# Queueing transposes ahead at the ends of the layers of a four-layer graph network, and halving its last output

## The chip, the cores and the metric

The kernel runs on one core of one Trainium2 chip. The metric is the device time of one launch, in microseconds (us). Three runs of the kernel before took 530.57, 530.88 and 531.29 us. A core has engines that run side by side, each through a queue of instructions of its own in a fixed order, and wait for one another on semaphores: TensorE (PE in the profile) multiplies matrices into PSUM, DVE (VectorE) and ACT (ScalarE) do elementwise work, GpSimd (POOL) also, and SyncE (SP) issues most DMAs.

## The reference

A graph of 512 nodes with 512 features each and 16384 edges goes through four layers, each of the form x = x + layer(relu(layernorm(x))). In short:

```python
h = relu(layernorm(x));  x = x + transformer(h, edges)        # layer 0
h = relu(layernorm(x))
x = x + h @ wc + mean_over_edges(h @ wn) + bias               # layer 1
h = relu(layernorm(x))
for e in range(4):                                            # layer 2, experts; top 2 of 4 are kept
    t = relu(A @ h @ Wl[e, 0] + bl[e, 0] + h @ Wr[e, 0])      # A: mean over incoming edges
    t = relu(A @ t @ Wl[e, 1] + bl[e, 1] + t @ Wr[e, 1])
    x = x + gate[e] * t
h = relu(layernorm(x))
x = x + relu(S @ (h @ W + b))                                 # layer 3, S: normalized adjacency with loops
```

All of it is float32. The edge sums are done as products with a dense 512 x 512 matrix of edge counts.

## The kernel before

The nodes lie in four blocks of 128 rows, one row to a partition: `xs` holds x, `h` the normalized rows. A product of `h` with a weight needs `h` transposed, so `turn` (L189) transposes a block on TensorE, four pieces of 128 x 128 into one PSUM bank (L193), and ACT copies the bank into `hT` (L194). All four layers use the one `hT`.

In layer 0 the order of TensorE, DVE and ACT is written out by hand (`manual_schedule`, L480 to L695). Its end is `ff_up(1, 6)`, then the down projections `ff_down` of blocks 2 and 3 (banks `pf22`, `pf23`, L690 to L695), the residual sums on DVE (L381) and the normalizations `norm2_a`, `norm2_b`, `norm2_c` (L433 to L445). The PSUM pools are `ps_mm` and `ps_x`; `banks` says from which the next bank is taken. From L702 on there is one pool of eight banks.

In layers 1 and 3 a scheduler orders the instructions of each engine from the order in the program and the dependences. In layer 2, from L956 on, only TensorE's order is by hand.

Layer 1 (L736 to L754): for blocks 0 and 1, then for 2 and 3, two turns, then `pbe` = h @ wn for both (its high part is cast by ACT, L709, its low part is left by DVE, L710), then `pal` = h @ wc for both (added to `xs` on DVE, L747). GpSimd adds the bias to `xs` (L739). Then four edge sums `psu` (L751), each followed by an add on DVE (L752), a normalization `norm_relu` (DVE and ACT, L158 to L184), and a low part `hs` (L754).

Layer 2 begins with, for each block, a turn, the gate product `pg` (L764) and eight products `pag` for the edge sums of `h` (L767). Sums of quarters of `hT`, of the edge sums and of the weights follow on DVE (`right_sums`, `left_sums`), for a scheme that makes a 2 x 2 block product from seven multiplications (`seven`). Weights are loaded by SP into five buffers, each as soon as its last reader is done. The last expert ends, for each block, with `po` (L950), `close` (an edge sum `pq` on TensorE, an add on DVE L907, a relu on ACT L909, an add into `xs` on DVE L910) and `norm_relu`.

Layer 3 (L978 to L1004): for each block a turn, `ph` = h @ W (L985), bias on DVE (L987), a scaled high part and a scaled whole on ACT (L989, L990), the low part on DVE (L991). Then the edge sums `pm` of all four blocks over source blocks 0 to 2 and then over 3 (L997), and for each block a relu on ACT (L1001), an add on DVE (L1003) and the output DMA on SP (L1004). `rm` and `o` are in pools of two buffers each.

Of the kernel before, what the change touches and what calls it, by code (L numbers as in the profile page):

```python
# [8 lines left out]
F32 = mybir.dt.float32  # L9
F16 = mybir.dt.float16  # L10
BF16 = mybir.dt.bfloat16
R = mybir.dt.float32r
I32 = mybir.dt.int32
AF = mybir.ActivationFunctionType
ALU = mybir.AluOpType
# [3 lines left out]
P = 128  # L19
N = 512  # L20
D = 512
E = 16384
NB = N // P
KB = D // P
# [4 lines left out]
NX = 4  # L29
# [7 lines left out]
def fast(  # L37
# [4 lines left out]
    nc = tc.nc  # L42
# [4 lines left out]
    rows = ctx.enter_context(tc.tile_pool(name="rows", bufs=2))  # L47
    ps_mm = tc.alloc_tile_pool(name="ps_mm", bufs=2, space=PSUM)
    ps_lo = tc.alloc_tile_pool(name="ps_lo", bufs=2, space=PSUM)
    ps_sc = tc.alloc_tile_pool(name="ps_sc", bufs=1, space=PSUM)  # L50
    banks = [(ps_mm, "mm"), (ps_mm, "mm"), (ps_lo, "lo")]
    taken = [0]

    def bank(name):
        pool, tag = banks[taken[0] % len(banks)]
        taken[0] += 1
        return pool.tile([P, 512], F32, tag=tag, name=name)
# [5 lines left out]
    xs = const.tile([P, NB, D], F32, name="xs")  # L63
# [34 lines left out]
    gw = const.tile([P, KB, NX], F32, name="gw")  # L98
# [22 lines left out]
    ident = const.tile([P, P], F32, name="ident")  # L121
# [9 lines left out]
    h = const.tile([P, NB, D], F32, name="h")  # L131
    hT = const.tile([P, KB, N], F32, name="hT")
# [53 lines left out]
    def norm_relu(blocks, name, first=None):  # L186
        norm_relu_end(blocks, name, norm_relu_begin(blocks, name), first)

    def turn(dst_t, src_t, b, name):  # L189

        p = bank(f"tp_{name}{b}")
        for k in range(KB):
            nc.tensor.transpose(p[:, k * P:(k + 1) * P], src_t[:, b, k * P:(k + 1) * P], ident)  # L193
        nc.scalar.copy(dst_t[:, :, b * P:(b + 1) * P], p.rearrange("p (k n) -> p k n", k=KB))  # L194

    def mm(p, pairs):
        for i, (a, c) in enumerate(pairs):
            nc.tensor.matmul(p, a, c, start=(i == 0), stop=(i == len(pairs) - 1))  # L198

    def blk(t, k, j):  # L200
        return t[:, k, j * P:(j + 1) * P]
# [16 lines left out]
    C = deg_p.tile([P, NB, N], R, name="C")  # L218
# [5 lines left out]
    W = N // 2  # L224
# [199 lines left out]
    def ff_up(hf, f):  # L424
        ff_up_out(hf, f, ff_up_mm(hf, f))
# [53 lines left out]
    ET = mybir.EngineType  # L479
    with tc.manual_schedule(engines={ET.PE, ET.DVE, ET.Activation}):  # L480
# [25 lines left out]
        for c in range(NCH):  # L506
# [16 lines left out]
            i, at = divmod(c - 17, 9)  # L523
            if 0 <= i < len(first):
                w, t, off, j, cols = first[i]
# [98 lines left out]
        p = ff_up_mm(0, 2)  # L624
# [8 lines left out]
        ps_x = tc.alloc_tile_pool(name="ps_x", bufs=4, space=PSUM, reuse_waits="tile")  # L633
# [4 lines left out]
        p = ff_up_mm(0, 6)  # L638
# [39 lines left out]
        p = ff_up_mm(1, 0)  # L678
# [8 lines left out]
        nc.vector.reciprocal(ideg_b, ideg_b)  # L687
        ff_up(1, 4)
        ff_up(1, 6)
        p2, p3 = bank("pf22"), bank("pf23")  # L690
        ff_down(2, p2, range(FB))
        y = residual(p2, 2, "y2")
# [14 lines left out]
    def split(hi, lo, full, copy):  # L707

        copy(hi, full)  # L709
        nc.vector.tensor_sub(lo, full, hi.bitcast(F32))  # L710
# [22 lines left out]

    pair = main.tile([P, 2, NB, D], F32, tag="pair", name="pair")
    beta = pair.bitcast(R)
    for blocks in ((0, 1), (2, 3)):  # L736
        for b in blocks:
            turn(hT, h, b, "h2_")
            nc.gpsimd.tensor_add(xs[:, b, :], xs[:, b, :], bias1_b)  # L739
        for b in blocks:  # L740
            p = bank(f"pbe{b}")
            mm(p, [(blk(hT, k, b), wns[:, k, :]) for k in range(KB)])
            split(beta[:, 0, b, :], beta[:, 1, b, :], p, nc.scalar.copy)
        for b in blocks:
            p = bank(f"pal{b}")
            mm(p, [(blk(hT, k, b), wcs[:, k, :]) for k in range(KB)])
            nc.vector.tensor_add(xs[:, b, :], p, xs[:, b, :])  # L747
    hs = main.tile([P, 2, NB, D], R, tag="hs", name="hs")
    for b in range(NB):
        p = bank(f"psu{b}")  # L750
        mm(p, [(blk(CT, j, b), beta[:, i, j, :]) for j in range(NB) for i in range(2)])  # L751
        nc.vector.scalar_tensor_tensor(xs[:, b, :], p, icnt[:, b:b + 1], xs[:, b, :], op0=ALU.mult, op1=ALU.add)  # L752
        norm_relu((b,), "n2_", hs[:, 0, b, :])
        nc.vector.tensor_sub(hs[:, 1, b, :], h[:, b, :], hs[:, 0, b, :].bitcast(F32))  # L754

    ct_p.release()
    te_p = ctx.enter_context(tc.tile_pool(name="te_p", bufs=1, side="right", reuse_waits="tile"))
# [1 line left out]

    pg = bank("pg")  # L760
    pag = [bank(f"pag{k}") for k in range(KB)]
    for b in range(NB):
        turn(hT, h, b, "h3_")
        mm(pg[:, b * NX:(b + 1) * NX], [(blk(hT, k, b), gw[:, k, :]) for k in range(KB)])  # L764
        for k in range(KB):
            for i in range(2):
                nc.tensor.matmul(pag[k], blk(hs[:, i, :, :], b, k), C[:, b, :], start=(b == 0 and i == 0),  # L767
                                 stop=(b == NB - 1 and i == 1))

# [132 lines left out]
    def close(e, b, t, zz, gt):  # L904
        q = bank(f"pq{e}_{b}")
        mm(q, [(blk(C, a, b), zz[:, i, a, :]) for a in range(NB) for i in range(2)])
        nc.vector.scalar_tensor_tensor(t, q, ideg[:, b:b + 1], t, op0=ALU.mult, op1=ALU.add)  # L907
        r = rows.tile([P, D], F32, tag="r1", name=f"re{e}_{b}")
        nc.scalar.activation(r, t, AF.Relu, scale=gt[:, b, e:e + 1])  # L909
        nc.vector.tensor_add(xs[:, b, :], xs[:, b, :], r)  # L910
# [3 lines left out]
    def outer(e, w, gt):  # L914
        wl, wr, bl_b = w
        eT = eTs[e]
        L = left_sums(eT, scratch[:, 0:3], scratch[:, 3])

        zz = main.tile([P, 2, NB, D], R, tag="hs", name=f"zz{e}")

        def result_z(i, j, value):
            v = value(None)
            hi, lo = (zz[:, g, 2 * i:2 * i + 2, j * W:(j + 1) * W] for g in range(2))
            split(hi, lo, v, nc.scalar.copy)

        seven(f"pz{e}", [(L, wl)], copied, result_z)
        te = te_p.tile([P, NB, D], F32, tag="te", name=f"te{e}")
        if e < NX - 1:
            bias = [bl_b[:, None, j * W:(j + 1) * W].to_broadcast([P, 2, W]) for j in range(2)]

            def first_o(p):
                ts = []
                for j in range(2):
                    t = uu.tile([P, 2, W], F32, tag="u", name=f"u_b{e}_{j}")
                    nc.vector.tensor_add(t, p, bias[j])
                    ts.append(t)
                return ts

            def result_o(i, j, value):
                t = te[:, 2 * i:2 * i + 2, j * W:(j + 1) * W]  # L940
                if (i, j) == (0, 0):
                    nc.vector.tensor_add(t, value(None), bias[0])
                else:
                    value(t)

            seven(f"po{e}", [(L, wr)], first_o, result_o)
        for b in range(NB):
            if e == NX - 1:
                p = bank(f"po{e}_{b}")
                mm(p, [(blk(eT, k, b), wr[:, k, :]) for k in range(KB)])  # L950
                nc.vector.tensor_add(te[:, b, :], p, bl_b)
            close(e, b, te[:, b, :], zz, gt)
            if e == NX - 1:
                norm_relu((b,), "n3_")

    with tc.manual_schedule(engines={ET.PE}):  # L956
        a0, a1 = weights0(0), weights0(1)
# [14 lines left out]
        w3 = load_w(W3, "w3")  # L972
        b3_b = load_bc(b3, "b3_b")
        outer(3, o3, gt)

    for b in range(NB):  # L978
        nc.vector.tensor_add(blk(C, b, b), blk(C, b, b).bitcast(F32), ident)
        nc.vector.tensor_scalar(xs[:, b, :], xs[:, b, :], nanf[:, b:b + 1], None, op0=ALU.add)  # L980
    gs = main.tile([P, 2, NB, D], R, tag="hs", name="gs")
    for b in range(NB):
        turn(hT, h, b, "h4_")
        p = bank(f"ph{b}")
        mm(p, [(blk(hT, k, b), w3[:, k, :]) for k in range(KB)])  # L985
        t = rows.tile([P, D], F32, tag="r0", name=f"th{b}")
        nc.vector.tensor_add(t, p, b3_b)  # L987
        gg = rows.tile([P, D], F32, tag="r1", name=f"gg{b}")
        nc.scalar.activation(gs[:, 0, b, :], t, AF.Copy, scale=isd[:, b:b + 1])  # L989
        nc.scalar.activation(gg, t, AF.Copy, scale=isd[:, b:b + 1])  # L990
        nc.vector.tensor_sub(gs[:, 1, b, :], gg, gs[:, 0, b, :].bitcast(F32))  # L991
    pm = [bank(f"pm{b}") for b in range(NB)]
    for a in ((0, 1, 2), (3,)):
        for b in range(NB):
            for c in a:
                for i in range(2):
                    nc.tensor.matmul(pm[b], blk(C, c, b), gs[:, i, c, :], start=(c == 0 and i == 0),  # L997
                                     stop=(c == NB - 1 and i == 1))
    for b in range(NB):
        r = rows.tile([P, D], F32, tag="r1", name=f"rm{b}")  # L1000
        nc.scalar.activation(r, pm[b], AF.Relu, scale=isd[:, b:b + 1])  # L1001
        o = rows.tile([P, D], F32, tag="r0", name=f"o{b}")
        nc.vector.tensor_add(o, r, xs[:, b, :])  # L1003
        nc.sync.dma_start(out[b * P:(b + 1) * P, :], o)  # L1004


    ps.release()

# [429 lines left out]
```

## Time and profile before

| what | value |
|---|---|
| runs, median | 530.88 us |
| the profiled execution's own time | 528.97 us |
| its span in the profile | 527.2 us |
| TensorE busy | 482.4 us, 92% |
| DVE busy | 358.2 us, 68% |
| ACT busy | 154.9 us, 29% |
| GpSimd busy | 8.3 us, 2% |
| chain that ended last, by engine | PE 70%, DVE 20%, ACT 5%, DMA 2%, issue 2% |

The span runs from the first to the last instruction in the profile; the run's own time has a little more around it. The profile cuts the span into 40 slices and gives the busy tenths of each engine in each (9 is 90% or more), and the clock that TensorE was granted. A timeline lists the instructions of an engine in order: start, duration, engine, line, operation, output and input, shapes, and in brackets how long the engine had been idle before and which instruction ended that. The ends of matmuls are modelled, and pipelined groups overlap a little, so steps are best measured from start to start. Layer 1 begins at 207.66 us, layer 2 at about 248, its experts' products at 262.04, layer 3 at 488.76.

### The profile page before, as it was taken

What the parts mean: (1) busy time and instruction counts of PE and PEld (TensorE: products, weight loads), DVE (VectorE), ACT (ScalarE), POOL (GpSimd) and SP (SyncE); (2) the same over time, 40 slices, a digit from 0 to 9 for tenths busy, and PEclk for the clock granted to TensorE, in tenths of its full rate; (3) what the DMA queues carried; (4) which work ended last, traced back from release to release, by engine and by line L of the source; (5) the groups of instructions that cost most, each with busy time, mean ns of one, the idle gap of its engine ahead of it and who ended that gap; (6) DMA issues with size and microseconds to landing.
All of it is one profiled execution on the core that took longest, in us unless ns stands there. A gap on an engine that the chain in (4) does not pass through costs nothing.

```text
span 527.2 us, 5637 instructions
## 1 busy us (share of the span) xinstructions
PE 482.4 (92%) x2159; PEld 358.0 (68%) x2159; DVE 358.2 (68%) x726; ACT 154.9 (29%) x315; POOL 8.3 (2%) x14
## 2 busy tenths in 40 slices
PE   2999889696999998999999999999999999999791
PEld 1798556354774673446888888888888888875451
DVE  8898999998987868818564457823783256558521
ACT  3886443332521321212402121112202120223421
POOL 2000000000000000100000000000000000000000
PEclk9999999989999999999999999999999999999997
DMA  7820202200003054112004042203131040000002
GB/s 250 287 75 1 80 2 79 80 21 0 1 22 119 0 171 149 60 63 98 0 1 159 1 159 81 80 1 129 43 104 45 6 154 0 1 1 0 1 2 83
DMA packets 18354, 34.42 MB, mean 65 GB/s; under 512 B 1512, under 2 KB 1808, under 8 KB 18320
## 3 DMA queue, kind: packets, MB, share of 16 engines
q1 hardware_dynamic: 17504, 32.61, 18.4%
q10 hardware_dynamic: 816, 1.38, 0.7%
q8 instruction: 19, 0.31, 0.2%
q14 instruction: 15, 0.12, 0.1%
HBM read 32.93 MB, written 1.05 MB: 64 GB/s over the span
## 4 chain that ended last, share of the span: by engine, by line
PE 70%; DVE 20%; ACT 5%; DMA 2%; issue 2%; ACTq 0%; DVEq 0%
PE pe_b L805 8%; PE pff L198 5%; PE pe_a L805 5%; PE pe_c L805 5%; PE pq L198 5%; PE pz_b L805 3%; PE po_b L805 3%; PE pbe L198 3%; PE pqk L198 3%; PE pwo L377 3%; PE pf L430 3%; PE pal L198 3%; DVE m L304 2%; PE ph L198 2%; PE pz_a L805 2%; PE po_a L805 2%
## 5 line engine op out<-in xcount | busy, mean ns | idle before, releaser
L811 DVE TENSOR_TENSOR u_pe<-pe_b,u_first 128x512 f32<-128x512 f32 x12 | 8.3, 692 | 53.6 <-PE pe_b L805 53.6
L198 PE MATMUL pq<-zz,C 128*128 128x512 f32 x128 | 33.1, 412 | 0.0
L271 DVE TENSOR_SCALAR ohs<-iota_h,src_f,dw_i 128x256 bf16<-128x256 f16 x104 | 28.9, 340 | 1.7 <-PE cps L273 1.6
L198 PE MATMUL pff<-hT,w 128*128 128x256 f32 x128 | 28.6, 381 | 0.7 <-issue 0.7
L198 PEld LDWEIGHTS pq<-zz,C 128*128 128x128 f32 x128 | 24.1, 188 | 7.2 <-issue 1.9
L273 PE MATMUL cps<-ohs,ohd 128*128 128x256 bf16 x104 | 19.5, 289 | 9.7 <-DVE ohs L271 9.7
L430 PE MATMUL pf<-w,ffT 128*128 128x512 f32 x64 | 28.1, 592 | 0.0
L909 ACT ACTIVATE re<-te,gt 128x512 f32<-128x512 f32 x16 | 11.6, 723 | 54.9 <-DVE te L907 54.9
L871 ACT ACTIVATE eT<-u_pe,vecs 128x256 f32<-128x256 f32 x24 | 10.9, 500 | 56.4 <-DVE u_pe L811 56.4
L198 PEld LDWEIGHTS pff<-hT,w 128*128 128x128 f32 x128 | 24.1, 190 | 5.0 <-issue 1.7
L273 PEld LDWEIGHTS <-ohd 128*128 128x128 f16 x128 | 15.7, 145 | 13.6 <-DVE ohd L266 7.9
L299 PE MATMUL psc<-qT,kT 64*128 64x256 f32 x128 | 17.8, 421 | 4.2 <-DVE s L310 4.2
L430 PEld LDWEIGHTS pf<-w,ffT 128*128 128x128 f32 x64 | 12.0, 190 | 13.9 <-issue 13.6
L304 DVE TENSOR_REDUCE m<-psc 128x256 f32<-128x2048 f32 x8 | 18.3, 2286 | 1.7 <-PE cps L273 1.2
L310 DVE TENSOR_TENSOR s<-psc,m 128x1024 f32<-128x1024 f32 x16 | 18.8, 1216 | 0.1
L348 PE MATMUL aps<-s,v 128*64 128x256 f32 x128 | 15.8, 390 | 3.0 <-DVE nt_l L145 3.0
L299 PEld LDWEIGHTS psc<-qT,kT 64*128 64x128 f32 x128 | 13.2, 204 | 7.8 <-issue 6.5
L709 ACT CAST zz<-u_pz 128x512 fp32r<-128x512 f32 x12 | 7.4, 618 | 37.7 <-DVE u_pz L811 37.7
L338 DVE TENSOR_TENSOR s<-s,r 128x2048 f32<-128x2048 f32 x8 | 18.3, 2286 | 0.1
L198 PE MATMUL ph<-w,hT 128*128 128x512 f32 x32 | 14.8, 605 | 3.4 <-ACT hT L194 3.4
L311 ACT ACTIVATE s<-s 128x1024 f32<-128x1024 f32 x16 | 16.8, 1054 | 3.3 <-DVE s L310 2.9
L910 DVE TENSOR_TENSOR xs<-xs,re 128x512 f32<-128x512 f32 x16 | 11.0, 691 | 8.0 <-ACT re L909 8.0
(264 smaller groups left out, 1047.2 us busy)
## 6 DMA issues: line engine op xcount, KB each, us to landing
wr<-in_L_gnn_Wr_dram SPq DMA_DIRECT2D x8, 1024.0 KB
wl<-in_L_gnn_Wl_dram SPq DMA_DIRECT2D x8, 1024.0 KB
w<-in_L_gnn_W_dram SPq DMA_DIRECT2D x5, 1024.0 KB
wk<-in_L_gnn_Wk_dram SPq DMA_DIRECT2D x1, 1024.0 KB
wq<-in_L_gnn_Wq_dram ACTq DMA_DIRECT2D x1, 1024.0 KB
wv<-in_L_gnn_Wv_dram SPq DMA_DIRECT2D x1, 1024.0 KB
wo<-in_L_gnn_Wo_dram SPq DMA_DIRECT2D x1, 1024.0 KB
bl_b<-in_L_gnn_bl_dram SPq DMA_DIRECT2D x4, 256.0 KB
```

Of the source, the lines that this page charges most:

```text
L198: nc.tensor.matmul(p, a, c, start=(i == 0), stop=(i == len(pairs) - 1))
L271: nc.vector.tensor_scalar(ohs, iota_h, src_f[:, c:c + 1], dw_f[:, c:c + 1], op0=ALU.is_equal, op1=ALU.mult)
L273: nc.tensor.matmul(cps, ohd[0][:, :, c % 8], ohs, start=(c == 0), stop=(c == NCH - 1))
L299: nc.tensor.matmul(psc[i][:, 4 * g + j, :], kT[o:o + HD, j, b * P:(b + 1) * P], qT[o:o + HD, j, cols], start=True, stop=True)
L304: nc.vector.tensor_reduce(m, psc[i].rearrange("p h n -> p n h"), axis=AX.X, op=ALU.max)
L310: nc.vector.tensor_sub(s[:, g, :], psc[i][:, g, :], m[:, None, :].to_broadcast([P, 4, W]))
L311: nc.scalar.activation(s[:, g, :], s[:, g, :], AF.Exp, scale=1.0 / 8.0)
L338: nc.vector.tensor_mul(s, s, rz[i].to_broadcast([P, H, W]))
L348: nc.tensor.matmul(aps[hf][j // 2][o:o + HD, j % 2, :], v[:, b, (2 * j + g) * HD:(2 * j + g + 1) * HD], s[:, 4 * g + j, :], start=(b == 0 ...
L377: nc.tensor.matmul(p, blk(qT, k, b), wo[:, k, :], start=(k == 0), stop=(k == KB - 1))
L430: nc.tensor.matmul(p, ffT[b // 2][:, f, c:c + P], w2[f // 4][:, f % 4, :], start=(f == 0), stop=(f == FB - 1))
L805: nc.tensor.matmul(p[:, m, :], l[i][:, k, m * P:(m + 1) * P], r[i][:, k, :], start=fresh, stop=(k == 1), skip_group_check=True)
```

## The change

In layer 0 the turns of blocks 0 and 1 for layer 1 are put after `ff_up(1, 6)`, ahead of the down projections of blocks 2 and 3, in banks of `ps_mm`. Layer 1 gets a TensorE order by hand: `beta_of(0)`, turn 2, `beta_of(1)`, `alpha_of(0)`, `alpha_of(1)`, turn 3, and so on; the bias is added on DVE in `alpha_of`. At its end turn 0 for layer 2 stands between the edge sums of blocks 2 and 3, turn 1 after that of block 3; turns 2 and 3 stand after the `pag` products of blocks 0 and 1, also by hand. In the last expert turn 0 for layer 3 stands after `po` of block 2, turn 1 after `close` and `norm_relu` of block 2. Layer 3 moves under the order by hand: turn 2, `ph` 0 and 1, turn 3, `ph` 2 and 3; the edge sums of blocks 0 and 1 over sources 0 to 2, then over 3, each followed by its output; then those of blocks 2 and 3 whole. The final rows `o` lie in the pool `uu` (six buffers), and those of block 3 are made in two halves of 256 columns, whose DMAs go out on SP and on ACT. The products, their number and their operands are the same. In the list of DVE's instructions of the built program, the four bias adds come after `norm_relu`'s first small step of each block in layer 0's end; the other steps keep their order but for a few small ones.

```diff
         ff_up(1, 4)
         ff_up(1, 6)
+        banks[:] = [(ps_mm, "mm")]
+        turn(hT, h, 0, "h2_")
+        turn(hT, h, 1, "h2_")
+        banks[:] = [(ps_x, "x")]
         p2, p3 = bank("pf22"), bank("pf23")
         ff_down(2, p2, range(FB))
...
-    for blocks in ((0, 1), (2, 3)):
-        for b in blocks:
-            turn(hT, h, b, "h2_")
-            nc.gpsimd.tensor_add(xs[:, b, :], xs[:, b, :], bias1_b)
-        for b in blocks:
-            p = bank(f"pbe{b}")
-            mm(p, [(blk(hT, k, b), wns[:, k, :]) for k in range(KB)])
-            split(beta[:, 0, b, :], beta[:, 1, b, :], p, nc.scalar.copy)
-        for b in blocks:
-            p = bank(f"pal{b}")
-            mm(p, [(blk(hT, k, b), wcs[:, k, :]) for k in range(KB)])
-            nc.vector.tensor_add(xs[:, b, :], p, xs[:, b, :])
...
+    def beta_of(b):
+        p = bank(f"pbe{b}")
+        mm(p, [(blk(hT, k, b), wns[:, k, :]) for k in range(KB)])
+        split(beta[:, 0, b, :], beta[:, 1, b, :], p, nc.scalar.copy)
+
+    def alpha_of(b):
+        nc.vector.tensor_add(xs[:, b, :], xs[:, b, :], bias1_b)
+        p = bank(f"pal{b}")
+        mm(p, [(blk(hT, k, b), wcs[:, k, :]) for k in range(KB)])
+        nc.vector.tensor_add(xs[:, b, :], p, xs[:, b, :])
+
+    def gamma_of(b):
         p = bank(f"psu{b}")
         mm(p, [(blk(CT, j, b), beta[:, i, j, :]) for j in range(NB) for i in range(2)])
         nc.vector.scalar_tensor_tensor(xs[:, b, :], p, icnt[:, b:b + 1], xs[:, b, :], op0=ALU.mult, op1=ALU.add)
         norm_relu((b,), "n2_", hs[:, 0, b, :])
         nc.vector.tensor_sub(hs[:, 1, b, :], h[:, b, :], hs[:, 0, b, :].bitcast(F32))
 
+    with tc.manual_schedule(engines={ET.PE}):
+        beta_of(0)
+        turn(hT, h, 2, "h2_")
+        beta_of(1)
+        alpha_of(0)
+        alpha_of(1)
+        turn(hT, h, 3, "h2_")
+        beta_of(2)
+        beta_of(3)
+        alpha_of(2)
+        alpha_of(3)
+        for b in range(NB - 1):
+            gamma_of(b)
+        turn(hT, h, 0, "h3_")
+        gamma_of(3)
+        turn(hT, h, 1, "h3_")
...
-    for b in range(NB):
-        turn(hT, h, b, "h3_")
-        mm(pg[:, b * NX:(b + 1) * NX], [(blk(hT, k, b), gw[:, k, :]) for k in range(KB)])
...
+    with tc.manual_schedule(engines={ET.PE}):
+        for b in range(NB):
+            mm(pg[:, b * NX:(b + 1) * NX], [(blk(hT, k, b), gw[:, k, :]) for k in range(KB)])
+            for k in range(KB):
+                for i in range(2):
+                    nc.tensor.matmul(pag[k], blk(hs[:, i, :, :], b, k), C[:, b, :], start=(b == 0 and i == 0),
+                                     stop=(b == NB - 1 and i == 1))
+            if b < 2:
+                turn(hT, h, b + 2, "h3_")
...
                 nc.vector.tensor_add(te[:, b, :], p, bl_b)
+                if b == 2:
+                    turn(hT, h, 0, "h4_")
             close(e, b, te[:, b, :], zz, gt)
             if e == NX - 1:
                 norm_relu((b,), "n3_")
+                if b == 2:
+                    turn(hT, h, 1, "h4_")
...
+    def out_of(p, b, parts):
+        r = rows.tile([P, D], F32, tag="r1", name=f"rm{b}")
+        o = uu.tile([P, 2, W], F32, tag="u", name=f"o{b}").rearrange("p m n -> p (m n)")
+        n = D // parts
+        for i in range(parts):
+            c = slice(i * n, (i + 1) * n)
+            nc.scalar.activation(r[:, c], p[:, c], AF.Relu, scale=isd[:, b:b + 1])
+            nc.vector.tensor_add(o[:, c], r[:, c], xs[:, b, c])
+            q = (nc.sync, nc.scalar)[i]
+            q.dma_start(out[b * P:(b + 1) * P, c], o[:, c])
...
-    for b in range(NB):
-        turn(hT, h, b, "h4_")
-        p = bank(f"ph{b}")
...
-    for a in ((0, 1, 2), (3,)):
         for b in range(NB):
-            for c in a:
-                for i in range(2):
-                    nc.tensor.matmul(pm[b], blk(C, c, b), gs[:, i, c, :], start=(c == 0 and i == 0),
-                                     stop=(c == NB - 1 and i == 1))
...
+        turn(hT, h, 2, "h4_")
+        weighted(0, w3, b3_b, gs)
+        weighted(1, w3, b3_b, gs)
+        turn(hT, h, 3, "h4_")
+        weighted(2, w3, b3_b, gs)
+        weighted(3, w3, b3_b, gs)
+        pm = [bank(f"pm{b}") for b in range(NB)]
+        for b in range(2):
+            sums_of(pm[b], b, range(NB - 1), gs)
+        for b in range(2):
+            sums_of(pm[b], b, (NB - 1,), gs)
+            out_of(pm[b], b, 1)
+        for b in (2, 3):
+            sums_of(pm[b], b, range(NB), gs)
+            out_of(pm[b], b, b - 1)
```

`weighted` holds the steps of `ph` to the low part of layer 3 as they were, `sums_of` the products of `pm`.

More of the change, by code (lines that the diff above doesn't have):

```diff
@@ L761, in fast @@
     pag = [bank(f"pag{k}") for k in range(KB)]
-    for b in range(NB):
-        turn(hT, h, b, "h3_")
-        mm(pg[:, b * NX:(b + 1) * NX], [(blk(hT, k, b), gw[:, k, :]) for k in range(KB)])
-        for k in range(KB):
-            for i in range(2):
-                nc.tensor.matmul(pag[k], blk(hs[:, i, :, :], b, k), C[:, b, :], start=(b == 0 and i == 0),
-                                 stop=(b == NB - 1 and i == 1))
+    with tc.manual_schedule(engines={ET.PE}):
[7 more added lines that the diff above has]
+                turn(hT, h, b + 2, "h3_")
     def quarter(t, a, b):
@@ L954, in outer, with weighted, sums_of @@
                 norm_relu((b,), "n3_")
+                if b == 2:
+                    turn(hT, h, 1, "h4_")
+    def weighted(b, w3, b3_b, gs):
+        p = bank(f"ph{b}")
+        mm(p, [(blk(hT, k, b), w3[:, k, :]) for k in range(KB)])
+        t = rows.tile([P, D], F32, tag="r0", name=f"th{b}")
+        nc.vector.tensor_add(t, p, b3_b)
+        gg = rows.tile([P, D], F32, tag="r1", name=f"gg{b}")
+        nc.scalar.activation(gs[:, 0, b, :], t, AF.Copy, scale=isd[:, b:b + 1])
+        nc.scalar.activation(gg, t, AF.Copy, scale=isd[:, b:b + 1])
+        nc.vector.tensor_sub(gs[:, 1, b, :], gg, gs[:, 0, b, :].bitcast(F32))
+    def sums_of(p, b, some, gs):
+        for c in some:
+            for i in range(2):
+                nc.tensor.matmul(p, blk(C, c, b), gs[:, i, c, :], start=(c == 0 and i == 0),
+                                 stop=(c == NB - 1 and i == 1))
+    def out_of(p, b, parts):
[8 more added lines that the diff above has]
+            q.dma_start(out[b * P:(b + 1) * P, c], o[:, c])
     with tc.manual_schedule(engines={ET.PE}):
@@ L974, in fast @@
         outer(3, o3, gt)
[L978 to L982, printed above, removed]
-        turn(hT, h, b, "h4_")
-        p = bank(f"ph{b}")
[L985 to L992, printed above, removed]
-    for a in ((0, 1, 2), (3,)):
-        for b in range(NB):
-            for c in a:
-                for i in range(2):
-                    nc.tensor.matmul(pm[b], blk(C, c, b), gs[:, i, c, :], start=(c == 0 and i == 0),
-                                     stop=(c == NB - 1 and i == 1))
[L999 to L1004, printed above, removed]
+        gs = main.tile([P, 2, NB, D], R, tag="hs", name="gs")
+        for b in range(NB):
+            nc.vector.tensor_add(blk(C, b, b), blk(C, b, b).bitcast(F32), ident)
+            nc.vector.tensor_scalar(xs[:, b, :], xs[:, b, :], nanf[:, b:b + 1], None, op0=ALU.add)
+        turn(hT, h, 2, "h4_")
[13 more added lines that the diff above has]
+            out_of(pm[b], b, b - 1)
     ps.release()
```

## The prediction

> **What bounds the kernel now.** I read the slices of the page first, then TensorE's timeline around each end of a layer, then the chain that ended last, then DVE's and ACT's timelines where TensorE stood still.
>
> ```profile
> PE   2999889696999998999999999999999999999791
> PEclk9999999989999999999999999999999999999997
> ```
>
> Each slice is 13.2 us. From slice 12 to 37 TensorE is full at a full clock, so only its holes and what follows it are worth anything. Between 272 and 467 us it is idle 0.8 of 195 us: layer 2's experts offer nothing, and a shift of their start is a shift of their end. The holes lie where a block is transposed (L193), in TensorE's timeline (start, duration, operation; in brackets idle before and who ended it):
>
> ```profile
> 207.66 0.60 PE L193 MATMUL tp_h<-ident,h 128*128 128x128 f32 x4
> 210.13 0.66 PE L193 MATMUL tp_h<-ident,h 128*128 128x128 f32 x4 [1.87 <-DVE y L381]
> 211.22 7.13 PE L198 MATMUL pbe<-wns,hT 128*128 128x512 f32 x16 [0.44 <-ACT hT L194]
> ...
> 225.06 1.04 PE L193 MATMUL tp_h<-ident,h 128*128 128x128 f32 x8
> 226.34 7.13 PE L198 MATMUL pbe<-wns,hT 128*128 128x512 f32 x16 [0.24 <-ACT hT L194]
> ...
> 248.29 0.66 PE L193 MATMUL tp_h<-ident,h 128*128 128x128 f32 x4 [0.52 <-ACT h L182]
> 249.62 1.05 PE L198 MATMUL pg<-gw,hT 128*128 128x4 f32 x8 [0.67 <-ACT hT L194]
> ```
>
> Here is the end of layer 2, same columns:
>
> ```profile
> 488.76 0.60 PE L193 MATMUL tp_h<-ident,h 128*128 128x128 f32 x4
> 490.27 3.70 PE L198 MATMUL ph<-w,hT 128*128 128x512 f32 x8 [0.92 <-ACT hT L194]
> 493.81 0.60 PE L193 MATMUL tp_h<-ident,h 128*128 128x128 f32 x4
> 495.50 3.70 PE L198 MATMUL ph<-w,hT 128*128 128x512 f32 x8 [1.08 <-ACT hT L194]
> ```
>
> Every hole is the same: transpose, wait for ACT's copy into hT, go on. And the tail, on all engines:
>
> ```profile
> 516.48 1.29 ACT L1001 ACTIVATE rm<-pm,isd 128x512 f32<-128x512 f32 x2 [0.24 <-DVE o L1003]
> 519.20 1.30 DVE L1003 TENSOR_TENSOR o<-rm,xs 128x512 f32<-128x512 f32 x2 [2.20 <-DMA out_dram<-o]
> ```
>
> The third final add waits 2.20 us until the first output has landed, because `o` has two buffers.
>
> [...] beside GpSimd's 1.27 us bias add (L739) a 128x1 DVE multiply (L145) took 1.25 us instead of 0.15. [...] the trace granted 1.00 across the 1.87 us hole. [...] The trace has issues at the start of 0.39 to 0.46 us on ACT and 0.38 to 0.43 on SP.
>
> **Part by part.** Times are on the clock of the profile before. A transpose group costs TensorE 0.37 us when other work follows (252.48 to the next matmul at 252.84).
>
> *1, into layer 1.* Before: from 207.66 to the first gamma sum (psu) at 240.17 are 32.51 us. The work is two pairs of pbe at 6.97, two of pal at 6.86, four turns at 0.37: 29.14. So 3.37 are saved if no wait is left; psu starts at 236.80. Waits, one by one. Turns 0 and 1 now stand ahead of the down projection (194): h of both was done by 188.7, and ACT's copies precede work that it waits for till 203.9, so they are hidden. They hold up pf22 and pf23 by 0.74. pf22's reader on DVE started at 202.10 because it stood behind weight sums that waited 5.83 us for a load; 0.74 later pf22 ends at 201.8, still ahead. The two loads (wl, wr on SP) that wait for pf22's and pf23's weights go out 0.74 later; block 3's normalization stands behind their sums on DVE, and is due at 222.4. DVE's queue walked through (four bias adds of 0.68 come from GpSimd, four collisions of 1.1 go, three weight sums of the second expert move behind block 3's scale) has h of block 3 at 219.7: 2.7 in hand; were they used up, TensorE would wait one for one. Block 2's turn is due at 211.9, h is there at 209.8. No wait.
>
> *2, out of layer 1.* Before, psu start to the first product of layer 2 (262.04) took 21.87: 7.48 psu, 12.8 turns, gates and pag, rest waits. Now TensorE's order is fixed: psu 0, 1, 2, turn 0, psu 3, turn 1. The price is DVE's chain:
>
> ```profile
> 242.24 0.75 DVE L752 SCALAR_TENSOR_TENSOR xs<-psu,icnt,xs 128x512 f32<-128x512 f32 x1
> ...
> 247.34 0.14 DVE L149 TENSOR_TENSOR rs_n<-nt_n,r_n 128x1 f32<-128x1 f32 x1
> ```
>
> From psu 0's end to the scale are 5.1 us, to h (ACT 247.52 to 248.24) 6.0. The queue up to the scale holds the same instructions after the change, so h of block 0 comes at 238.87+6.0=244.9. psu 2 ends at 236.80+5.61=242.41: TensorE waits 2.54. Turn to 245.32, psu 3 to 247.19. h of block 1 needs on DVE the hi/lo difference of block 0 (waits for ACT until 245.6), then eight small steps: scale 247.3, h 248.05. TensorE waits 0.86, with pag of block 0 queued behind it though its operands are ready. Then all is ready in time: turn, pg 3.4, pag 7.9, two turns 0.75, end 260.48. Behind the wait for turn 0 stand psu 3, whose adds come after both scales in DVE's queue, turn 1 and pg. Against 262.04 stages 1 and 2 save 1.56: stage 2 gives back 1.8. Bounds: the same chain without other blocks between took 4.6 (474.66 to 479.23): 1.4 less wait; one more instruction pair ahead of each scale: 1.4 more.
>
> *3, out of layer 2.* Before, the last `po` but one ended at 481.59 and ph 3 at 508.55. Now: turn 0 at once (h at 479.23) to 481.96, pq 2 to 483.83, turn 1 waits for h at 484.41 (0.62), to 484.82; po 3, pq 3 (3.43+1.87) to 490.12. ACT's queue has the hT copy of block 1 ahead of block 2's relu L909: xs of block 2 comes at 486.3 instead of 485.20, h at 490.9 instead of 489.75; turn 2 waits 0.83, to 491.32. Two ph (3.43) to 498.18; block 3's relu stands behind block 2's hT copy (492.1), h at 497.75, just in time. Turn, two ph: 505.41. Saved 3.14. The sums pm (32 x 0.243 = 7.78) wait 0.1 for block 3's low half; their end goes from 516.28 to 513.46: 2.82 saved.
>
> *4, the end.* Before, 516.28 to the last add's end 520.50: 4.22. Now two half relus (0.47 each, from ffT's 128x256 row; eT's says 0.50), then one half add: 128x128 took 0.28, 128x512 0.69, I take 0.42. The end is 514.82: 1.36, saved 2.86. With buffers of their own the first three outputs wait for nobody, and no work stands behind the last DMA on ACT. From the last add to the span's end were 6.70; of that the two last outputs, 512 KB, moved in about 1.4 us. Now 256 KB go last, in two issues: bounds 6.0 and 7.1 (issues in series), I take 6.3, saved 0.4.
>
> The sum is 1.56+2.82+2.86+0.40 = 7.64. Span 527.2 to 519.6; the profiled run 528.97 to 521.3. The runs' median of 530.88 lies 1.91 above that run, and I move it by the same: **523.2**.
>
> **Rivals.**
> *A, more waits than walked.* The fixed order pays each late h one for one, and 0.6, 0.8 and 0 in stage 3, 2.5 and 0.9 in stage 2 have little in hand. 1.4 more in stage 2 and 1.4 in stages 3 and 4 give 526.0. For: ACT's copies stand ahead of relus. Against: the same instructions, same durations.
> *B, the turns gain nothing,* only the tail does (the change doesn't do what it says: a turn queued ahead waits on h instead of on its copy). 530.88-3.3 = 527.6. For: the waits of stage 2. Against: blocks 0 and 1 in layer 0 and block 0 in layer 2 are ready by 2 to 5 us.
> *C, slower.* DVE takes psu 0 only after the second expert's weight sums, which wait for a load issued when pbe 3 ends. Before: issue 233.50, sums from 238.95 after 1.25 of waiting, psu 0 taken at 242.24, no slack. The turn now pinned ahead of psu 3 pays each us of a later landing. It decides from 7.6 us on: a load of 13 us instead of 5.4; at 10 us later the time is 533.2. Against: the DMA queues are empty then (0.00 busy at 220 to 234).
>
> **Chances.** Forecast (521.0 to 525.0) 0.64; A (to 527.0) 0.19; B 0.07; better than 521.0 0.03 (short chain in stage 2, short closing); C 0.07, of it 0.04 slower and 0.03 near no change. The range 521.0 to 527.0 leaves out 0.17. About 0.2%, 1.1 us, is what a measurement of this kernel can tell from no change; faster 0.93, same 0.03, slower 0.04.
>
> **What would show it.** In the changed profile: psu starts 3.4 us earlier; TensorE's transposes of layer 1's end show waits of about 2.5 and 0.9 on ACT's h, and the first product of layer 2 comes at 260.5. Layer 2's length is unchanged. L910's add of block 2 in the last expert is about 1 us later in its block, ph runs in pairs, pm ends near 512, the last two adds are halves with no DMA wait, and 6.3 us close. Wrong if turn 0 of layer 1's end waits over 4 us, if pbe 0 does not follow pf23 at once, or if the closing is above 7.

## The result, and the profile after

Four runs of the changed kernel took 521.31 to 522.26 us, median **522.03**; four of the kernel before, run beside them, took 530.57 to 531.60, median 531.09. The ratio is 0.9827 (95% interval 0.9810 to 0.9844). The profiled executions took 522.04 and 528.97 us, spans 520.4 and 527.2: in the profiles the change is worth 6.93 us (7.64 forecast), in the medians 9.06.

The slices of the page after; each is 13.0 us now, and the last one of TensorE holds 3 tenths instead of 1:

```profile
PE   2999889697999999998999999999999999999993
PEclk9999999979999999999999999999999999999998
```

TensorE's timeline of the changed kernel from the end of layer 0 to the first product of layer 2 (start, duration, operation; in brackets the idle time before and who ended it):

```profile
193.79 1.04 PE L193 MATMUL tp_h<-ident,h 128*128 128x128 f32 x8
194.66 13.90 PE L430 MATMUL pf<-w,ffT 128*128 128x512 f32 x32
208.40 3.60 PE L198 MATMUL pbe<-wns,hT 128*128 128x512 f32 x8
...
236.34 6.16 PE L198 MATMUL psu<-pair,CT 128*128 128x512 f32 x24
244.88 0.66 PE L193 MATMUL tp_h<-ident,h 128*128 128x128 f32 x4 [2.38 <-ACT h L182]
245.30 2.87 PE L198 MATMUL psu<-pair,CT 128*128 128x512 f32 x8
248.02 1.11 PE L193 MATMUL tp_h<-ident,h 128*128 128x128 f32 x4
...
261.24 1.89 PE L828 MATMUL pe_a<-hT,wr 128*128 128x256 f32 x8
```

From 193.79 to 242.5 no line has a bracket: every hole of layer 1's beginning is filled. Then comes the one wait that the new order makes, 2.38 us. After it something is odd: the edge sum of block 3 takes 2.87 us, where 8 of the 24 before it take 2.05; the next transposes take 1.11 instead of 0.60 to 0.66. The windows view of the same kernel (window and its length, TensorE's busy time and instructions in it, granted clock, then the DMA's share and GB/s) tells why:

```profile
245.00:246.00 1.00, 1.00 (x7) 1.00 0.00 0
246.00:247.00 1.00, 1.00 (x5) 0.68 0.00 0
247.00:248.00 1.00, 1.00 (x3) 0.50 0.00 0
...
249.00:250.00 1.00, 1.00 (x8) 0.62 0.00 0
```

The clock fell to a half within the second of these windows and was back within the last: from 246.36 to 249.76, for 3.4 us, TensorE had half its clock. In the profile before, these microseconds were at 1.00. On DVE, the chain that prices the wait (L756 is L752 of before):

```profile
238.80 0.75 DVE L756 SCALAR_TENSOR_TENSOR xs<-psu,icnt,xs 128x512 f32<-128x512 f32 x1
...
243.93 0.14 DVE L149 TENSOR_TENSOR rs_n<-nt_n,r_n 128x1 f32<-128x1 f32 x1
...
248.20 0.75 DVE L756 SCALAR_TENSOR_TENSOR xs<-psu,icnt,xs 128x512 f32<-128x512 f32 x1 [0.92 <-PE psu L198]
```

5.13 us from the add to the last small step, 5.10 before: the chain was moved, not changed. Its last line shows DVE waiting for the stretched sum. Then the end of layer 2 on TensorE:

```profile
480.75 0.60 PE L193 MATMUL tp_h<-ident,h 128*128 128x128 f32 x4
481.11 2.10 PE L198 MATMUL pq<-zz,C 128*128 128x512 f32 x8
483.61 0.66 PE L193 MATMUL tp_h<-ident,h 128*128 128x128 f32 x4 [0.40 <-ACT h L182]
...
490.16 0.66 PE L193 MATMUL tp_h<-ident,h 128*128 128x128 f32 x4 [0.60 <-ACT h L182]
490.65 7.03 PE L198 MATMUL ph<-w,hT 128*128 128x512 f32 x16
```

and the tail, the halves on ACT and DVE and the second DMA queue; no add waits for a landing:

```profile
512.58 0.84 ACT L1006 ACTIVATE rm<-pm,isd 128x256 f32<-128x256 f32 x2 [1.17 <-PE pm L997]
513.08 0.79 DVE L1007 TENSOR_TENSOR o<-rm,xs 128x256 f32<-128x256 f32 x2 [0.95 <-ACT rm L1006]
513.90 0.37 ACTq L1009 DMA_DIRECT2D out_dram<-o  x1
```

### The profile page after: what moved, and what is told of

It is laid out like the page before. It is cut to its first block, busy times and chain, and to the rows that moved or that the text cites. A ratio compares the mean times of both kernels' runs of the same rounds, so it can differ in the third digit from the quotient of the medians.

```text
span 520.4 us, 5638 instructions
## 1 busy us (share of the span) xinstructions
PE 482.4 (93%) x2159; PEld 358.9 (69%) x2159; DVE 356.5 (68%) x731; ACT 155.8 (30%) x316; POOL 2.8 (1%) x10
## 3 DMA queue, kind: packets, MB, share of 16 engines
HBM read 32.93 MB, written 1.05 MB: 65 GB/s over the span
## 4 chain that ended last, share of the span: by engine, by line
PE 74%; DVE 18%; ACT 3%; issue 2%; DMA 1%; ACTq 0%; DVEq 0%
PE pe_b L828 8%; PE pff L198 5%; PE pe_a L828 5%; PE pf L430 5%; PE pe_c L828 5%; PE pq L198 5%; PE pz_b L828 3%; PE po_b L828 3%; PE pqk L198 3%; PE pwo L377 3%; PE pbe L198 3%; PE ph L198 3%; PE cps L273 2%; DVE m L304 2%; PE pz_c L828 2%; PE po_a L828 2%
## 5 line engine op out<-in xcount | busy, mean ns | idle before, releaser
L828 PE MATMUL pe_b<-sums,wr 128*128 128x256 f32 x64 | 16.4, 379 | 0.0
```

The source lines that it names most:

```text
L828: nc.tensor.matmul(p[:, m, :], l[i][:, k, m * P:(m + 1) * P], r[i][:, k, :], start=fresh, stop=(k == 1), skip_group_check=True)
```

## The experiments

My theory before the experiments: the gain is a sum of four stages that don't touch each other, less the wait at layer 1's end and the 3.4 us at half clock that, by the theory, this wait causes. The rivals: turns queued ahead only move waits, the tail does it all; the clock's fall has another cause; and, for the 2 us between profile and medians, the waits for output landings vary, or the clock does. The twelve kernels ran on three chips in groups of four, each with the kernel before (medians 530.95, 530.26 and 530.21), so ratios compare best:

| kernel | median (runs) | ratio, 95% interval |
|---|---|---|
| e1_before | 531.06 (528.08 to 533.10) | 1.0014 (0.9994 to 1.0034) |
| e2_layer1 | 524.03 (523.29 to 524.78) | 0.9870 (0.9842 to 0.9897) |
| e4_tail | 526.18 (525.93 to 527.90) | 0.9920 (0.9890 to 0.9950) |
| e8_layer3 | 527.47 (525.34 to 529.55) | 0.9936 (0.9913 to 0.9960) |
| e3_end1 | 519.75 (519.02 to 523.61) | 0.9813 (0.9777 to 0.9848) |
| e5_fill | 521.63 (521.34 to 521.79) | 0.9830 (0.9799 to 0.9861) |
| e6_turn1late | 520.88 (520.71 to 521.14) | 0.9817 (0.9786 to 0.9847) |
| e7_whole | 521.58 (521.08 to 521.98) | 0.9828 (0.9797 to 0.9859) |
| e9_both | 520.69 (518.88 to 520.80) | 0.9801 (0.9776 to 0.9826) |
| e10_bothwhole | 519.33 (517.49 to 520.03) | 0.9787 (0.9761 to 0.9812) |
| e11_twobufs | 519.87 (519.57 to 520.98) | 0.9810 (0.9787 to 0.9833) |
| e12_begin1old | 525.08 (523.64 to 525.44) | 0.9898 (0.9876 to 0.9919) |

The medians carry noise of their own, so each profile was also cut at the same events. Stage 1 runs from the first down projection of block 2 (`pf22`) to the first edge sum (`psu`), stage 2 to the first product of layer 2, stage 3 to the first `pm`, stage 4 to the end of the last add; then the closing, to the span's end. Where the two turns stand ahead of `pf22`, they cost 0.87 us more before stage 1 starts (193.79 to 194.66).

| kernel | stage 1 | 2 | 3 | 4 | closing |
|---|---|---|---|---|---|
| before | 45.85 | 22.26 | 246.22 | 12.24 | 6.70 |
| e1_before | 45.46 | 22.25 | 246.24 | 13.26 | 6.90 |
| e2_layer1 | 41.68 | 22.25 | 246.24 | 12.57 | 4.85 |
| e4_tail | 45.44 | 22.27 | 246.18 | 10.31 | 6.34 |
| e8_layer3 | 45.38 | 23.82 | 243.22 | 12.54 | 5.85 |
| after | 41.68 | 24.90 | 243.18 | 9.45 | 6.53 |
| e3_end1 | 41.68 | 22.26 | 243.24 | 9.44 | 6.07 |
| e5_fill | 41.68 | 24.06 | 243.22 | 9.46 | 6.26 |
| e6_turn1late | 41.68 | 24.85 | 242.40 | 9.46 | 6.29 |
| e7_whole | 41.68 | 24.07 | 243.21 | 9.57 | 5.78 |
| e9_both | 41.68 | 23.85 | 242.41 | 9.46 | 5.98 |
| e10_bothwhole | 41.68 | 22.25 | 242.42 | 9.56 | 5.46 |
| e11_twobufs | 41.68 | 24.08 | 243.25 | 9.58 | 4.66 |
| e12_begin1old | 45.46 | 24.05 | 243.22 | 9.45 | 6.09 |

**e1_before**, no edit.

> The kernel before once more, unchanged. The change moved the medians by 9.06 us but the two profiled executions only by 6.93; the profiled execution of the kernel before lay 2 us under its runs' median. If that one execution was a lucky draw, this profile's own time lies near 531 and its span near 529, and the holes of the trace are up to 2 us larger somewhere. If profiling itself makes this program faster by 2 us, it lies near 529 again.

Its profiled execution took 530.38. It differs from the first profile in a window of half clock from 125.6 to 129.1, which the first one lacks, and by 1.0 us in stage 4. Ahead of stage 1 this profile is 0.56 us longer, which is all that the window can be seen to have cost. The 1.0 us in stage 4 are waits for landings; there were two of them here, where the first profile had one of 2.20:

```profile
519.64 0.69 DVE L1003 TENSOR_TENSOR o<-rm,xs 128x512 f32<-128x512 f32 x1 [2.50 <-DMA out_dram<-o]
521.01 0.69 DVE L1003 TENSOR_TENSOR o<-rm,xs 128x512 f32<-128x512 f32 x1 [0.68 <-DMA out_dram<-o]
```

So the first profile was a favourable draw, and both the clock and the landings vary from execution to execution. More on this with e9 and e11 and in the next section.

**e2_layer1**: the diff's hunks for layers 0 and 1 up to the last `alpha_of`, nothing else.

> Layer 1's beginning alone: the turns of blocks 0 and 1 ahead of the down projections and layer 1's order by hand up to the last h @ wc product; everything from the edge sums on as before. My theory (the change is a sum of four stages that do not touch each other): the first edge sum starts at 236.4 and the end moves one for one, -3.4 us against before, so about 527.6 in the runs and a span of 523.8. Rival (turns queued ahead only move a wait to the next late block): less than 1 us.

6.9 us less, twice what was expected. The stage table takes it apart. Stage 1 is 3.3 less turns included (45.85 to 41.68 and 0.87), and stages 2 and 3 don't react: the gain moves through one for one, as the theory has it. But the closing is 1.85 shorter than before's, for no reason in the diff, and most of the rest is the gap between before's profile and its median.

**e4_tail**: on the kernel before,

```diff
-        nc.scalar.activation(r, pm[b], AF.Relu, scale=isd[:, b:b + 1])
-        o = rows.tile([P, D], F32, tag="r0", name=f"o{b}")
...
+        o = uu.tile([P, 2, W], F32, tag="u", name=f"o{b}").rearrange("p m n -> p (m n)")
+        n = D // (2 if b == 3 else 1)
```

> The tail alone: output rows in buffers of their own, the last block's in halves, the rest as before. Theory: two adds and a wait less at the end (2.86) and a closing shorter by 0.2 to 0.4 give -3.1 to -3.3 us. Rival B of the forecast (the turns gain nothing, the tail does it all): -7 to -9 us, as the whole change.

4.8 less, where 3.1 to 3.3 were expected. In the profile 1.9 of it is in stage 4 and 0.4 in the closing; 0.7 lies ahead of the tail, where the edit does not reach, and most of the rest is again the gap between before's profile and its median. Rival B (the tail does it all) is out, since the whole change is worth 9, and e2 and the next kernel gain without a new tail.

**e8_layer3**: on the kernel before, the two turns in the last expert, and turns and `ph` of layer 3 by hand.

> Layer 3 a block ahead alone: turns 0 and 1 in the last expert, ph in pairs by hand; layer 1 and the order and buffers of the output sums as before. Theory: ph ends 3.1 us earlier, the sums pm 2.8, and all of 2.8 shows at the end: -2.8. Rival: the tail, which waits 2.20 us for an output's landing, swallows some of it; less than 1.5.

3.5 less (0.40% to 0.87%), and stage 3 is 3.00 shorter in its profile; stage 4, with its wait for a landing, is 0.3 longer and swallows little. But stage 2, in code that the edit leaves as it was, is 1.56 longer: this execution had half clock from 249.91 to 253.32. So such a window falls on the old order too.

**e3_end1**: the changed kernel with this undone:

```diff
-        for b in range(NB - 1):
-            gamma_of(b)
-        turn(hT, h, 0, "h3_")
-        gamma_of(3)
-        turn(hT, h, 1, "h3_")
```

the four `gamma_of` stand after the block, and the turns, `pg` and `pag` are left to the scheduler as before.

> The changed kernel with the end of layer 1 (edge sums, turns for layer 2, gates, pag) in the order of before, all else as changed. Theory (the fixed order there costs 1.8 us of waits by the walk and 0.76 more by the clock): the first product of layer 2 comes at about 258.7 instead of 261.24, the clock stays at 1.00, and the time is 2.0 to 2.5 us less than the changed kernel's 522.0. Rival (the order by hand there is worth something, since the turns of blocks 2 and 3 hide behind pag): within 0.5 us of the changed kernel or slower.

Nearly as expected: 22.26 instead of 24.90 in stage 2, 2.3 us less by the medians, and 1.8 less than e7 (below), which ran on the same chip and is the changed kernel but for the halves. The intervals of the ratios overlap, since two of e3's six runs took 521.20 and 523.61; it is the stages that agree: 22.25 to 22.27 in every profile of the old order without a window, 24.05 and more in every one of the new. The order by hand there is the one part of the change that costs time.

By the medians the parts do not add up: 6.9, 4.8 and 3.5 (e2, e4, e8) less the 2.3 of e3 would be 12.9, and the whole change brought 9.06. In the stages they do: 3.3, 1.9 and 3.0 less 2.6 is 5.6, the four stages of the change give 6.5, and the 0.9 between lies in stage 4, where the changed kernel has the sums block by block besides. A median of one part thus holds some 2 us that are not the edit's.

**e5_fill**:

```diff
+        fill = bank("fill")
+        mm(fill, [(blk(CT, j, 2), beta[:, i, j, :]) for j in range(NB) for i in range(2)])
         turn(hT, h, 0, "h3_")
```

> The changed kernel plus one group of eight products (those of the third edge sum over again, into a bank whose content is used nowhere), put into TensorE's wait ahead of the first turn at layer 1's end. It adds 1.87 us of TensorE work into a wait of 2.4. Clock theory (the wait of 2.4 us made the clock fall to 0.50, which stretched the next 3 us): clock stays 1.00 from 244 to 252, psu 3 takes 1.87 instead of 2.72, first product of layer 2 at 260.5, time 0.5 to 0.8 less than the changed kernel in spite of more work. Rival (the clock's fall has another cause): the clock falls again in the same place, time the same or up to 0.3 more.

The clock stays at 1.00, stage 2 is 24.06, and 1.87 us more of work cost nothing: the wait ahead of turn 0 is 0.51 instead of 2.38, and turn 0 starts 8.53 us after the first edge sum, 8.54 in the changed kernel. The wait's end is set by DVE's chain, not by TensorE. It doesn't prove the clock theory, though, because of e7.

**e7_whole**: `out_of(pm[b], b, b - 1)` becomes `out_of(pm[b], b, 1)`.

> The changed kernel with the last block's output rows whole (one relu, one add, one DMA on SyncE). Theory: the relu 0.87 and add 0.69 instead of two halves in step cost 0.3 more, and the closing is 0.2 longer: +0.4 to +0.8 us. Rival: the second DMA issue costs as much as the halves save: no change within 0.2.

No loss: the ratio is that of the changed kernel (0.9828 and 0.9827), as the rival said. Its reason, the cost of a second issue, isn't shown: stage 4 is 0.12 longer, the closing 0.75 shorter, and closings vary without an edit too. And by chance this execution shows the wait of layer 1's end without the window of half clock, in unchanged code:

```profile
246.11 0.66 PE L193 MATMUL tp_h<-ident,h 128*128 128x128 f32 x4 [2.38 <-ACT h L182]
246.52 2.10 PE L198 MATMUL psu<-pair,CT 128*128 128x512 f32 x8
249.24 0.66 PE L193 MATMUL tp_h<-ident,h 128*128 128x128 f32 x4 [0.62 <-ACT h L182]
```

The same 2.38 us of idle, then a sum of 2.10 us instead of 2.87, and a second wait of 0.62. Stage 2 has 24.07, 24.08 and 24.05 in the three profiles without the window (e7, e11, e12) and 24.90 and 24.85 in the two with it (after, e6): the window costs 0.8 there.

**e6_turn1late**:

```diff
+                if b == 3:
+                    turn(hT, h, 1, "h4_")
             close(e, b, te[:, b, :], zz, gt)
...
-                if b == 2:
-                    turn(hT, h, 1, "h4_")
```

> The changed kernel with the turn of block 1 for layer 3 moved from behind the third block's close to behind po of block 3. Theory: TensorE's wait of 0.40 ahead of it goes, and block 2's relu on ACT no longer stands behind a copy into hT, so its turn waits less than 0.60: the time falls by 0.4 to 1.0 us. Rival: block 3's relu then stands behind the same copy and the wait reappears at turn 3: no change within 0.2.

TensorE's timeline of this kernel, against the one after above:

```profile
481.05 2.11 PE L198 MATMUL pq<-zz,C 128*128 128x512 f32 x8
483.00 3.60 PE L198 MATMUL po<-wr,eT 128*128 128x512 f32 x8
486.43 0.60 PE L193 MATMUL tp_h<-ident,h 128*128 128x128 f32 x4
486.79 2.10 PE L198 MATMUL pq<-zz,C 128*128 128x512 f32 x8
489.28 0.66 PE L193 MATMUL tp_h<-ident,h 128*128 128x128 f32 x4 [0.39 <-ACT h L182]
```

The wait of 0.40 is gone, `po` starts at once, and block 2's relu on ACT comes at 483.98 instead of 484.78, no longer behind a copy, so the wait of 0.60 is 0.39. Stage 3 is 0.8 shorter, the median 1.15 less than the changed kernel's and 0.7 less than e7's on the same chip. The wait does not come back at turn 3.

**e9_both** (e3 and e6 together) and **e10_bothwhole** (e7 too).

> The changed kernel with both improvements found so far: the end of layer 1 in the order of before, and layer 3's turn of block 1 behind po of block 3. If the stages are independent their gains add: 2.3 and 1.1 us off the changed kernel's 522.0, so 518.5 to 519. If the two share something, it stays at the better one's 519.7.

> The same with the last block's rows whole. The changed kernel with whole rows took 0.45 us less than the changed kernel where 0.4 to 0.8 more had been expected: its closing, from the last add to the end, was 5.8 us against 6.1 to 6.5. If halves really cost something there (two issues on two queues), this is 0.2 to 0.6 less than the version with halves; if that was chance, it is within 0.2 or slower.

e9 shows what the others hide. Its runs took 520.80, 520.70 and 520.69 at a mean clock of 0.983, and 518.88 and 519.05 at 0.990: one program, two times. The profiled execution is the first of them, and its windows show two stretches of half clock that e10's profile has not, from 126 and from 249 us. (The one from 102 is in all fourteen profiles, beginning between 101.7 and 104.7.)

```profile
102.00:103.00 1.00, 0.00 (x0) 0.62 0.00 0
...
126.00:127.00 1.00, 1.00 (x8) 0.56 0.00 0
...
129.00:130.00 1.00, 1.00 (x9) 0.73 0.00 0
...
249.00:250.00 1.00, 1.00 (x4) 0.50 0.00 0
...
252.00:253.00 1.00, 1.00 (x5) 0.79 0.00 0
```

A mean of 0.62, between 1.00 and 0.50, puts the fall at 102.24; the others lie at 126.12 and 249.00. The distances are 23.88 and 122.88 us, 7 and 36 times 3.413; in after and e6 the two falls lie 143.36 apart, 42 times that. The two extra stretches of e9 lasted 3.42 us each, the one from 102 lasted 6.82. The one at 249 made stage 2 23.85 instead of 22.25. Both gains are there (stage 2 as in e3 but for this window, stage 3 as in e6), but in three of five runs 1.8 us more hide them, with the lower clock. e10, at 0.990, took 517.49 and 517.98, 0.9 to 1.6 less than e9 at 0.990: whole rows are no worse than halves. That they are better isn't shown, since closings vary by as much. e10 has the best median of all, 2.1% under the kernel before; its interval still touches that of the change.

**e11_twobufs** and **e12_begin1old**.

```diff
-        o = uu.tile([P, 2, W], F32, tag="u", name=f"o{b}").rearrange("p m n -> p (m n)")
+        o = rows.tile([P, D], F32, tag="r0", name=f"o{b}")
...
-            out_of(pm[b], b, b - 1)
+            out_of(pm[b], b, 1)
```

> The changed kernel with the output rows back in the pool of two buffers (and whole). Open is why the runs of the kernel before lie between 528.0 and 533.1 while those of the changed kernel lie within 1 us. Tail theory: the waits for an output's landing vary from run to run, so this kernel's runs spread over 3 us or more again and its median is 2 to 4 us above the changed kernel. Clock theory (extra windows of 3.4 us at half clock after holes in TensorE's work at the ends of the layers): the spread stays near 1 us and only the wait for the landing, 1 to 1.5 us, is added.

> The changed kernel with the beginning of layer 1 as before (turns of blocks 0 and 1 not queued ahead, the scheduler's order, bias on GpSimd), all else as changed. Walk of the forecast: +3.4 us, 525.4. Clock theory: before's hole there (two waits of 1.87 and 0.44 us within 3 us) halves the clock for a window in some executions, so the runs spread over 2 us or more and the median rises by 4 to 5.5. Tail theory: +3.4 and no more spread than the changed kernel.

e11's last two adds do wait for a landing again:

```profile
511.98 1.36 DVE L1007 TENSOR_TENSOR o<-rm,xs 128x512 f32<-128x512 f32 x2 [2.17 <-DMA out_dram<-o]
```

and yet its runs spread over 1.4 us only, and it is no slower than the changed kernel (2.2 us less by the medians, 0.9 by the ratios, whose intervals overlap): the tail theory fails for this order of the sums, and the 1 to 1.5 us that I expected to pay did not come. The wait covers time in which the last sums weren't ready anyway: from the last sum's end to the last add's it is 1.47 us against 1.34. Under the old order nothing covers it, so that e11 can't tell whether landings spread the runs of the kernel before; e1 shows that they moved one profile by 1.0. e11's profiled execution took 519.74 against 522.04; 0.8 of that is the window of half clock that it happens not to have, 1.9 the closing. e12 gives back 3.05 us by the medians, 3.8 by the ratios, and spreads over 1.8: near the 2.9 that its stage 1 shows (45.46 against 41.68 and 0.87) and the 3.4 of the walk, not the larger loss that the clock theory gave; that part of it was wrong.

## Why the prediction was right, and where it was wrong

The time lies in the range, 1.2 us below the forecast, and the mechanism was in the main the forecast one: the holes closed where the blocks were ready, and the wait that the new order makes came where it was walked. That the number is so close is in part luck: the profiled run took 0.7 more than forecast, and the 1.91 then added for the median had no counterpart, since the changed kernel's profile lies at its median (522.04 and 522.03). Step by step, against before's profile:

- **Into layer 1**: 3.37 forecast, 3.44 measured (`psu` 239.78 to 236.34). All the walked slack held: no wait anywhere. The forecast's 240.17 is not a start in the trace but the last `pal` group's start plus 6.86; `psu` starts at 239.78, and the same shift on both sides leaves the difference as it is. Before's hole was larger in this profile (1.87) than in e1, e4, e8 and e12 (1.41 to 1.49); against those the step is worth 2.9.
- **Out of layer 1**: 1.8 given back forecast, 2.64 measured. Waits of 2.54 and 0.86 were forecast, 2.38 and 0.62 measured where the clock stayed up (e7), and stage 2 is then 24.07, 1.81 more than before. **The step that failed** is the clock: "the trace granted 1.00 across the 1.87 us hole", and I carried no term for less. That the walked waits would leave the clock alone was my estimate; no trace had shown it. In the profile after, the 3.41 us ahead of the fall (242.95 to 246.36) held 1.93 us of the wait, and the next 3.41 were granted 0.50. In e11's, the same length from 243.11 (41 times 3.413 after its own fall at 103.16) held 1.86, and the next was granted 1.00. The term that was missing is 0.8 us, in those executions in which the clock fell. It is no mark of the new order, though: of the eight profiles with the old order at this place two had such a window (e8, e9) and paid 1.6; of the five with the new one and its wait unfilled two had it (after, e6) and paid 0.8. The other six of the old order, before's among them, had none.
- **Out of layer 2**: waits of 0.62, 0.83 and 0 forecast, 0.40, 0.60 and none measured; 2.82 forecast from the first product to the end of the sums, 2.95 measured (254.24 to 251.29). The forecast's own terms give 2.99: 505.41, a wait of 0.1 and sums of 7.78 end at 513.29, not at 513.46. "Every hole is the same" was read too widely as well: of the lines it stands under, the 1.87 was ended by DVE's `y` and the 0.52 by ACT's `h`, not by a copy into `hT`.
- **The end**: 1.36 forecast from the last sum to the last add, 1.34 measured, so the size was exact. The credit was not. e11 shows that buffers and halves bring 0.13 us of the 2.88; the rest comes from summing block by block, so that the earlier blocks' rows are done before the last sum. On the old order (e4) buffers and halves bring 1.9.
- **The closing**: 6.3 forecast, 6.53 measured, 0.17 less than before. Nothing shows that halves shorten it: with whole rows it was 5.78 (e7), 5.46 (e10) and 4.66 (e11).

The stages as measured add up to 3.44 - 2.64 + 2.95 + 2.88 + 0.17 = 6.80, the difference of the spans. That the median moved 2 us more is the other error of the forecast, in its last step: I moved the median "by the same". Why the runs of the kernel before lie 2 us above its first profile is settled only in part. Of 53 further executions, the 14 with a mean clock of 0.985 or more have a median of 529.1 us, the 39 below that one of 531.1. One window of 3.4 us at half clock takes at most 1.7 us of full clock, by my estimate 0.0032 in the mean over 527 us, so the lower mean fits an extra window. But the mean also counts the fall after the last product, where TensorE has no product left (7.5 us of it in the profile before, 4.4 after), and the 22 executions at 0.982 still spread from 529.58 to 531.93. In e1's profile 0.56 at most can be laid to the extra window, and 1.0 is the landings'. e2, with the old tail, spread over 1.5 us only, at a steady clock, which speaks for the clock; two runs of e12 at 0.982 took only 0.2 to 0.5 more than two of the four at 0.991, which speaks against it. So the clock goes with these times, and how much of the 2 us it makes and how much the landings stays open. The extra windows seen in e1 and e9 at 126 us lie in layer 0, in code that the change leaves alone; that the change makes them rarer isn't shown.

Rival A's extra waits did not come. Rival C's load landed in time: the weight sums waited 1.38 us for it (1.25 before), and psu 0's add followed at 238.80.

## What to carry to other kernels

Before pinning an order by hand, walk the consumer's queue: where the block isn't ready, each late microsecond is paid, and an order that the scheduler found may be better (here by 1.8 us). A wait on TensorE can cost more than its length: after the one of 2.38 or 2.39 us here the granted clock was 0.50 for 3.4 us in two of five profiles (after, e6), at 0.8 us more each. So compare profiles by stages cut at the same events, and look at the granted clock of each before explaining a microsecond. When a change bundles several edits at one place, undo them one at a time: the buffers and halves of this tail looked necessary and, under the new order of the sums, were worth 0.1 us.

## What was not expected of the hardware

That some profiles have 3.4 us at half clock at layer 1's end and others of the same code there have none. I laid each profile out in steps of 3.413 us (122.88 / 36, from e9), counted from its own fall of the clock near 102 us. At layer 1's end, the step ahead of the fall held 1.93 us of idle time of TensorE in after and 2.03 in e6; steps with 1.48, 1.73 and 1.86 in e7, e12 and e11 were followed by a clock of 1.00. No one length parts them in all places: in layer 0, in the step that begins between 122.2 and 123.1 us, 1.91 (e4) and 1.99 (e12) were followed by 1.00, and 2.14 (e9) and 2.36 (e1) by 0.50.

Idle time alone doesn't decide. In the steps from 245.97 (e4) and from 246.50 (e8), on the old order, TensorE was idle for the same 1.20 us and transposed for the same 0.66; e4's held 0.42 us of 4-column gate products and was followed by a clock of 1.00, e8's held 0.78 and was followed by 0.50. In e9, 0.92 of idle beside 1.05 of gate products was followed by 0.50 too. What decides is not shown.

The closing is not constant. From the end of the last packet of output to the end of the span it takes 2.0 us in e2 and e11, 4.1 in the changed kernel, and 5.0 in e1, which is the kernel before. Packets of the instruction queue (q14) fall into this time, but of the three that follow the last output in the changed kernel two begin after the span's end. Why the closing varies stays open.
